# First of two attention stages: row maximum subtracted by TensorE in PSUM, fp16 halves written in two copies, small products alternating between row tiles

## Chip, cores and metric

The kernel runs on one core of a Trainium2 chip. A time is the device time of one execution in microseconds (us), from the first to the last instruction plus what lies around them. The hardware profiler's record of one execution is what this text calls the trace; its span runs from the first to the last instruction.

## What is computed

The input x is (16, 256, 128) in fp32. It passes a windowed self-attention with residual ("first attention"), and then a stack of six layers, each of them a windowed causal attention with 16 heads of 64 and a gated feed-forward (GELU). Only the first attention is touched by the change. Cut to what matters:

```
xn  = layernorm(x)                                  # over the 128 channels
qkv = xn.reshape(64 windows, 64, 128) @ W_qkv       # 16 heads of 8
q, k = layernorm(q) * gamma + beta, layernorm(k) * gamma + beta
attn = softmax((q * 8/8) @ k.T)                     # 64 x 64 per window and head
x   = x + (attn @ v) @ W_proj + b_proj
x   = x + six_layers(layernorm(x))
```

## The kernel before, in words

**Stages of the first attention** (`first_attention`, L298 to L527). The 16 sequences are worked in 8 units of two sequences, that is 4 tiles of 128 tokens (two windows) each. A unit passes six stages: `stage_load` (row statistics by `row_stats`, four transposes on TensorE), `stage_qkv` (three products of 128x384 per tile, then the layernorm of q and k per head), `stage_heads` (q and k are split in an fp16 high half and an fp16 rest, both are written to `hl`, with the halves doubled so that one product of 32 rows holds high*high, high*rest and rest*high, and `hl` is transposed by a DMA), `stage_soft`, `stage_out` and `stage_norm` (second row statistics, transposes into `xg`, the input of the six layers). `stage_soft` and `stage_out` take half a unit (two tiles) at a time, so the first attention is a software pipeline of 16 half-steps, with the later stages of old units beside the early stages of new ones. The loop at the end (`for k in range(2 * NU + LN0)`) merges the stages by fixed offsets.

**In `stage_soft`** each tile has two groups `jj` of scores, one PSUM bank `ps` each. VectorE takes the maximum of the bank (L449) and subtracts it on the way into SBUF, `p0` (L450). ScalarE exponentiates a whole tile (L460) and writes the fp16 high half (L462), GpSimd writes the rest (L463), and a DMA transposes both to `pt` (L465). **In `stage_out`** TensorE multiplies by v (L481, 48 products per tile, all of window c = 0 and then all of c = 1, in two PSUM tiles `po`), VectorE divides by the sums (L483, L486), and TensorE transposes and projects (L494, L501).

**Order.** The kernel is written in the tile framework: its scheduler fixes, when the kernel is built, one order of instructions for each engine, and an engine starts nothing before the instruction ahead of it has started. Nothing in the first attention is pinned; the order follows priorities and the scheduler's own estimates. The six layers have their order on TensorE written out (`pin`). SBUF and PSUM of the first attention are released and used again by the six layers: `SPLIT0 = (2, 2, 2, 1, 1)` gives the PSUM banks of the pools pq, ps, po, py, pt of the first attention, `SPLIT = (2, 3, 2, 1)` those of the six layers, on the same eight banks in the same order. The last stages of the first attention and the first projections of the six layers (`stage_p`, TensorE line L292 with `bank<-wqkv,xhl`) overlap in time.

**The weights** of layer 0 are prepared beside the first attention (`weights(0, ...)`).

The two lines on the maximum before:

```python
V.tensor_reduce(nm, psf, AX.X, ALU.max)                                  # L449
V.tensor_tensor(p0[...], psf, nm.unsqueeze(2).to_broadcast([128, 8, 64]), ALU.subtract)   # L450
```

Of the kernel before, what the change touches and what calls it, by code (L numbers as in the profile page):

```python
# [31 lines left out]
LOAD_AT = 6  # L32
LOAD_T = 10
SPLIT = (2, 3, 2, 1)
SPLIT0 = (2, 2, 2, 1, 1)
USE = dict(p=0, t=1, w=1, s=2, f=3)
USE_V = (1, 2)
LQ0, LH0, LS0, LO0, LN0 = 2, 4, 6, 7, 9
# [18 lines left out]
def kernel(  # L57
# [28 lines left out]

    ident = const.tile([128, 128], F32, name="ident")
    make_identity(nc, ident)
    onesm = const.tile([128, 128], F32, name="onesm")
    G.memset(onesm, 1.0 / 128.0)  # L90
    center = const.tile([128, 128], F32, name="center")
# [203 lines left out]
        pin(T.transpose(*args))  # L295


    def first_attention(p1, p2, p3, pqp, psp0, pop, pyp, ptp=None):  # L298
        ptp = ptp or pyp
        def rsqrt(dst, src, scale):  # L300
            if dst.shape[1] != 128:
                S.activation(dst, src, AF.Ln, bias=epst, scale=scale)
# [13 lines left out]
        def row_stats(xt, pre):  # L316
            mu = p3.tile([128, 4], F32, name=f"{pre}mu")
            rs = p3.tile([128, 4], F32, name=f"{pre}rs")
            sq = p3.tile([128, 128], F32, name="sq0")
            for t in range(4):  # L320
                S.activation(sq, xt[:, t], AF.Copy, scale=-1.0 / 128.0, accum_out=mu[:, t : t + 1])
            for t in range(4):
                S.activation(sq, xt[:, t], AF.Square, bias=mu[:, t : t + 1], accum_out=rs[:, t : t + 1])
            rsqrt(rs, rs, 1.0 / 128.0)
            return mu, rs
# [20 lines left out]
        dma(gam, g0.partition_broadcast(128))  # L346
        dma(bet, be0.partition_broadcast(128))
        dma(bpt, bp0.partition_broadcast(128))
        pm = pqp.tile([128, 512], F32, name="pq")
        T.matmul(pm[:, 0:384], onesm, w0r, start=True, stop=True)  # L350
        V.tensor_tensor(w0r, w0r, pm[:, 0:384], ALU.subtract)
# [13 lines left out]
        def stage_load(u):  # L365
            if u:
                load_x(u)
            e = U[u]
            _, e.rs = row_stats(e.xt, "a")
            e.rv = p1.tile([128, 4], F32, name="rv")  # L370
            V.tensor_scalar(e.rv, e.rs, VPRE, None, ALU.mult)
            yield
            e.xnt = p1.tile([128, 2, 4, 128], FR, name="xnt")
            pt = ptp.tile([128, 4, 128], F32, name="pt" if ptp is not pyp else "py")
            for t in range(4):
                T.transpose(pt[:, t], e.xt[:, t], ident)
            S.copy(e.xnt[:, 0], pt)
            V.tensor_tensor(e.xnt[:, 1], pt, e.xnt[:, 0].bitcast(F32), ALU.subtract)
            G.tensor_tensor(e.xt, e.xt, bpt.unsqueeze(1).to_broadcast([128, 4, 128]), ALU.add)
            yield  # L380
# [26 lines left out]
        def stage_heads(u):  # L407
            e = U[u]
            e.hl = []
            for s in range(2):  # L410
                src = e.qk[:, :, s * 128 : s * 128 + 128].rearrange("p t (h d) -> p t h d", d=8)
                hl = p1.tile([128, 4, 16, 4, 8], HP, name=f"hl{s}")
                for t in range(4):
                    hi, lo = hl[:, t, :, 0], hl[:, t, :, 2 if s else 1]
                    S.copy(hi, src[:, t])
                    G.tensor_tensor(lo, src[:, t], hi, ALU.subtract)
                    if s:
                        V.tensor_copy(hl[:, t, :, 1:4:2], hl[:, t, :, 0:3:2])
                    else:
                        V.tensor_copy(hl[:, t, :, 2:4], hl[:, t, :, 0:2])  # L420
                tr = p2.tile([128, 4, 4, 128], HP, name=f"tr{s}")
                nc.sync.dma_start_transpose(
                    tr.rearrange("p t i q -> p (t i) q"), hl.rearrange("p t h a d -> p (t h a d)")
                )
                e.hl.append(tr)
                yield

        def stage_soft(u, n2):
            e = U[u]
            p0 = p2.tile([128, 2, 8, 128], F32, name="p0")  # L430
            for n in range(2):
                t = 2 * n2 + n
                for jj in range(2):
                    ps = psp0.tile([128, 4, 2, 64], F32, name="ps")
                    for i in range(4):
                        for c in range(2):
                            cols = slice(64 * c, 64 * c + 64)
                            for vp in range(2):
                                r = slice(64 * jj + 32 * vp, 64 * jj + 32 * vp + 32)
                                T.matmul(  # L440
                                    ps[64 * vp : 64 * vp + 64, i, c],
                                    e.hl[0][r, t, i, cols],
                                    e.hl[1][r, t, i, cols],
                                    start=True,
                                    stop=True,
                                )
                    nm = p2.tile([128, 8], F32, name="nm0", bufs=4)
                    psf = ps.rearrange("p i c k -> p (i c) k")
                    V.tensor_reduce(nm, psf, AX.X, ALU.max)  # L449
                    V.tensor_tensor(  # L450
                        p0[:, n, 4 * jj : 4 * jj + 4].rearrange("p i (c k) -> p (i c) k", c=2),
                        psf,
                        nm.unsqueeze(2).to_broadcast([128, 8, 64]),
                        ALU.subtract,
                    )
                    yield
            e.pt = {}
            for n in range(2):
                pf = p0[:, n]
                S.activation(pf, pf, AF.Exp)  # L460
                ph = p2.tile([128, 2, 8, 128], HP, name="ph")
                S.copy(ph[:, 0], pf)  # L462
                G.tensor_tensor(ph[:, 1], pf, ph[:, 0], ALU.subtract)  # L463
                e.pt[n] = p3.tile([128, 16, 128], HP, name="pt0", bufs=3)
                nc.sync.dma_start_transpose(e.pt[n], ph.rearrange("p l m k -> p (l m k)"))  # L465
                yield

        def stage_out(u, n2):
            e = U[u]
            for n in range(2):  # L470
                t = 2 * n2 + n
                pt0 = e.pt[n]
                v = v0[(4 * u + t) % NV0]
                o0 = p3.tile([128, 2, 8, 8], F32, name="o0")
                for c in range(2):
                    r = slice(64 * c, 64 * c + 64)
                    po = pop.tile([128, 8, 18], F32, name="po")
                    for gm in range(8):
                        p = gm % 4 * 2 + gm // 4
                        for q, (a, b) in enumerate(((0, 0), (0, 1), (1, 0))):  # L480
                            T.matmul(po[:, p], pt0[r, a * 8 + gm], v[r, b, p], start=(q == 0), stop=(q == 2))  # L481
                    rc = p3.tile([128, 8], F32, name="rc0")
                    V.reciprocal(rc, po[:, :, 16])  # L483
                    for hp in range(2):
                        h = slice(64 * hp, 64 * hp + 64)
                        V.tensor_tensor(  # L486
                            o0[h, c],
                            po[h, :, hp * 8 : hp * 8 + 8],
                            rc[h].unsqueeze(2).to_broadcast([64, 8, 8]),
                            ALU.mult,  # L490
                        )
                yield
                py = pyp.tile([128, 512], F32, name="py")
                T.transpose(py[:, 0:128], o0.rearrange("p c a b -> p (c a b)"), ident)  # L494
                ot0 = p3.tile([128, 128], F32, name="ot0")
                S.copy(ot0, py[:, 0:128])
                py = pyp.tile([128, 512], F32, name="py")
                for c in range(2):
                    r = slice(64 * c, 64 * c + 64)
                    for hp in range(2):  # L500
                        T.matmul(  # L501
                            py[r, 0:128],
                            ot0[r, hp * 64 : hp * 64 + 64],
                            wp[r, hp],
                            start=(hp == 0),
                            stop=(hp == 1),
                        )
                V.scalar_tensor_tensor(e.xt[:, t], py[:, 0:128], 1.0 / VPRE, e.xt[:, t], ALU.mult, ALU.add)
                yield

        def stage_norm(u):
# [6 lines left out]
            for t in range(4):  # L518
                S.activation(xn[:, t], e.xt[:, t], AF.Identity, bias=mu[:, t : t + 1], scale=rs[:, t : t + 1])
            yield  # L520
            pt = ptp.tile([128, 4, 128], F32, name="pt" if ptp is not pyp else "py")
            for t in range(4):
                T.transpose(pt[:, t], xn[:, t], ident)
            pb = pt.rearrange("p (b j) t -> p b (j t)", j=2)
# [40 lines left out]
    keep = ctx.enter_context(tc.tile_pool(name="keep", bufs=1))  # L565
    work = ctx.enter_context(tc.tile_pool(name="work", bufs=WB))

    identh = keep.tile([128, 128], HP, name="identh")
    V.tensor_copy(identh, ident)
    maskf = keep.tile([128, 256], F32, name="maskf")  # L570
    dma(maskf, masks)
    rowsb = keep.tile([128, 128], BF, name="rowsb")
# [445 lines left out]
```

## Time and profile before

| what | value |
|---|---|
| device time, median of 3 runs | 3251.98 us (3251.57 to 3252.38) |
| device time of the profiled execution | 3248.45 us |
| its span | 3246.6 us |
| last DMA transpose of the first attention has landed, first product of the six layers | 267.9 us, 269.2 us |
| last copy of the first attention into `xg` | 286.4 us |
| busy share of the span: PE, DVE, ACT, POOL | 93%, 80%, 73%, 77% |
| mean granted TensorE clock | 0.957 of full speed |

PE is TensorE's matmuls, PEld its weight loads, DVE is VectorE, ACT is ScalarE, POOL is GpSimd, SP issues DMAs. PEclk is the clock that the throttle granted to TensorE as a share of full speed. A table by stretches gives, for each stretch of the span, every engine's busy time and its number of instructions. A row of a group reads: line, engine, operation, output <- inputs, shapes, count | busy time, mean duration of one in ns | idle time of the engine just before, and who ended it. The first 290 us of the span hold the first attention, the rest the six layers.

### The profile page before, as it was taken

How to read it: one execution, taken by the hardware profiler on the slowest of the kernel's cores; microseconds unless marked ns; L12 is line 12 of the kernel's file. 1: busy time of each engine (PE TensorE's matmuls, PEld its weight loads, DVE VectorE, ACT ScalarE, POOL GpSimd, SP SyncE). 2: the span in 40 equal slices, each digit the busy share in tenths (PEclk: the TensorE clock that was granted, in tenths of full speed). 3: DMA queues.
4: the chain of work that ended last, by engine and by line, in shares of the span. 5: the costliest groups of instructions: out<-in, count | busy, mean ns of one | idle time of the engine just before them, and what ended most of it. 6: DMA issues, size and time to landing. Idle time of an engine off the chain costs nothing. (4 is left out here: it accounts for less than half of the span.)

```text
span 3246.6 us, 153222 instructions
## 1 busy us (share of the span) xinstructions
PE 3016.5 (93%) x67106; PEld 2111.2 (65%) x67106; DVE 2600.2 (80%) x4850; ACT 2379.4 (73%) x5034; POOL 2509.8 (77%) x2578
## 2 busy tenths in 40 slices
PE   4887999999999999999999999999999999999996
PEld 3665766666666666666666666666666666666664
DVE  7987888888788888788887788888788888777783
ACT  6877777777777777777777777777777777767773
POOL 5657988888888888888878888878888888877771
PEclk6558999999999999999999999999999999999998
DMA  4763444444344344344444344444444444443342
GB/s 110 133 130 81 100 102 102 84 85 94 83 102 102 84 85 94 83 102 102 84 85 94 83 102 102 84 85 95 83 105 99 84 85 95 80 100 89 92 92 52
DMA packets 622946, 302.98 MB, mean 93 GB/s; under 512 B 533447, under 2 KB 545733, under 8 KB 622277
## 3 DMA queue, kind: packets, MB, share of 16 engines
q1 hardware_dynamic: 622276, 293.18, 42.9%
q8 instruction: 528, 8.65, 1.1%
q14 instruction: 142, 1.16, 0.1%
HBM read 22.45 MB, written 4.19 MB: 8 GB/s over the span
## 5 line engine op out<-in xcount | busy, mean ns | idle before, releaser
L292 PE MATMUL bank<-wqkv,xhl 128*128 128x512 f16 x3456 | 1238.8, 381 | 8.7 <-ACT sq L653 8.3
L655 POOL TENSOR_TENSOR sum<-mc 128x512 f32<-128x512 f32 x768 | 994.5, 1298 | 256.2 <-DVE mc L644 251.2
L644 DVE TENSOR_TENSOR mc<-bank,tq 128x1024 f32<-128x1024 f32 x768 | 930.1, 1220 | 137.9 <-PE bank L295 128.9
L665 POOL TENSOR_TENSOR sum<-sum,r 128x512 f32<-128x512 f32 x768 | 797.3, 1059 | 32.0
L654 DVE TENSOR_REDUCE r<-sq 128x8 f32<-128x512 f32 x768 | 519.8, 682 | 295.1 <-ACT sq L653 288.1
L295 PE MATMUL bank<-ident,sum 128*128 128x128 f32 x3072 | 713.0, 273 | 23.6 <-DVE of L792 23.6
L797 POOL TENSOR_TENSOR ohl<-of,ohl 128x512 f16<-128x512 f32 x384 | 451.5, 1176 | 225.8 <-ACT ohl L796 225.1
L653 ACT ACTIVATE sq<-bank 128x512 f32<-128x512 f32 x768 | 457.2, 609 | 159.7 <-DVE mc L644 158.2
L295 PEld LDWEIGHTS bank<-ident,sum 128*128 128x128 f32 x3072 | 433.1, 141 | 175.9 <-issue 68.4
L292 PEld LDWEIGHTS <-xhl 128*128 128x128 f16 x3456 | 339.3, 98 | 185.6 <-issue 18.0
L796 ACT CAST ohl<-of 128x512 f16<-128x512 f32 x384 | 237.8, 619 | 283.8 <-DVE of L792 279.9
L292 PE MATMUL bank<-vb,pt 64*32 64x65 f32 x6144 | 389.9, 225 | 31.0 <-ACT pt L622 21.0
L292 PEld LDWEIGHTS bank<-vb,pt 64*32 64x32 f32 x6144 | 263.8, 106 | 191.4 <-ACT p L276 51.7
L295 PE MATMUL bank<-ident,p 128*128 128x128 f32 x1536 | 354.9, 273 | 0.0
L292 PE MATMUL bank<-v,pt 64*32 64x65 f32 x6144 | 320.0, 225 | 35.0 <-ACT gt L282 13.4
L292 PE MATMUL bank<-vw,pt 64*32 64x65 f32 x12288 | 338.1, 225 | 0.1
L292 PE MATMUL bank<-ot,wohl 128*128 128x128 f16 x4608 | 296.0, 222 | 4.5 <-DMA ot<-ohl 4.5
L792 DVE TENSOR_TENSOR of<-bank,rc 128x256 f32<-128x256 f32 x768 | 294.2, 417 | 1.6
L292 PE MATMUL bank<-kt,qt 64*32 64x64 f32 (+1 forms) x24576 | 283.4, 223 | 1.6 <-issue 1.6
L292 PEld LDWEIGHTS bank<-kt,qt 64*32 64x32 f32 x24576 | 255.0, 105 | 45.6 <-issue 45.5
L292 PEld LDWEIGHTS bank<-v,pt 64*32 64x32 f32 x6144 | 237.0, 106 | 66.4 <-ACT pt L622 21.2
L292 PEld LDWEIGHTS <-wohl 128*128 128x128 f16 x4608 | 262.9, 99 | 22.5 <-DMA ot<-ohl 4.7
(155 smaller groups left out, 5063.1 us busy)
## 6 DMA issues: line engine op xcount, KB each, us to landing
v<-vb SPq DMA_DIRECT2D x384, 130.0 KB
vw<-vb SPq DMA_DIRECT2D x384, 130.0 KB
vw<-vb SPq DMA_DIRECT2D x576, 65.0 KB
wraw<-in_L_ffn_Wqkv_dram SPq DMA_DIRECT2D x36, 256.0 KB
wraw<-in_L_ffn_Wo_dram SPq DMA_DIRECT2D x12, 256.0 KB
ot<-ohl SPq DMA_TRANSPOSE x192
xt<-in_L_attn_x_dram SPq DMA_DIRECT2D x8, 256.0 KB
r1d<-xt SPq DMA_DIRECT2D x8, 256.0 KB
```

The lines of the kernel that those rows point to most:

```text
L292: pin(T.matmul(*args, **how))
L295: pin(T.transpose(*args))
L644: V.tensor_tensor(prod, p4.unsqueeze(3).to_broadcast([128, 8, 2, 2, 32]), tq[:, s, d.j].unsqueeze(1).to_broadcast([128, 8, 2, 2, 32]), ALU ...
L653: S.activation(sq, pp.rearrange("p (h d) -> p h d", d=64), AF.Square)
L654: V.tensor_reduce(r[:, hb * 8 : hb * 8 + 8], sq, AX.X, ALU.add)
L655: G.tensor_tensor(mc, m2[:, :, 0], m2[:, :, 1], ALU.add)
L665: G.tensor_tensor(mc, mc, rb.unsqueeze(2).to_broadcast([128, 8, 64]), ALU.mult)
L792: V.tensor_tensor(of[:, :, a], po[a][:, :, 0:64], rc.unsqueeze(2).to_broadcast([128, 4, 64]), ALU.mult)
L796: S.copy(ohl[:, 0, h], of)
L797: G.tensor_tensor(ohl[:, 1, h], of, ohl[:, 0, h], ALU.subtract)
```

## The change

In the first attention only:

- `stage_soft`: the maximum is taken negated in fp16, and TensorE adds it to the scores in PSUM by a product with the fp16 identity (128x512, one per bank); ScalarE exponentiates straight from PSUM, a bank at a time. The fp16 high half is then written by VectorE instead of ScalarE. The two banks of a tile are filled alternately, by four row tiles of 32 instead of two. `ps` has three banks instead of two.
- `stage_heads`: the high half and the rest are each written twice in one instruction (a broadcast source of 256 elements); the VectorE copies that doubled them go. The scale of the scores moves from the exponent's input into gamma and beta (two small GpSimd products) and the activation's scale.
- `stage_out`: the products with v, and the projections, alternate between the two row tiles c; both windows are in one PSUM tile of two banks, `po`, of which there is one; the reciprocal and the two products after it take both windows at once.
- `row_stats`: the sum of the rows by one VectorE reduction and a small GpSimd product instead of four ScalarE passes; `rv` by GpSimd.
- The transposes `pt` of `stage_load` and `stage_norm` take their PSUM from the pool pq, which the projections of the first attention use, instead of a bank of their own: `SPLIT0 = (2, 3, 1, 1)`. `identh` is made at the start instead of after the first attention.

```diff
-SPLIT0 = (2, 2, 2, 1, 1)
+SPLIT0 = (2, 3, 1, 1)
...
-            for t in range(4):
-                S.activation(sq, xt[:, t], AF.Copy, scale=-1.0 / 128.0, accum_out=mu[:, t : t + 1])
+            V.tensor_reduce(mu, xt, AX.X, ALU.add)
+            G.tensor_scalar(mu, mu, -1.0 / 128.0, None, ALU.mult)
...
+        for g in (gam, bet):
+            G.tensor_scalar(g, g, SDIV**-0.5, None, ALU.mult)
...
-            V.tensor_scalar(e.rv, e.rs, VPRE, None, ALU.mult)
+            G.tensor_scalar(e.rv, e.rs, VPRE, None, ALU.mult)
...
-            pt = ptp.tile([128, 4, 128], F32, name="pt" if ptp is not pyp else "py")
+            pt = pqp.tile([128, 512], F32, name="pq").rearrange("p (t c) -> p t c", t=4)
...
+                hi, lo = (slice(0, 2), slice(2, 4)) if s else (slice(0, 3, 2), slice(1, 4, 2))
                 for t in range(4):
-                    hi, lo = hl[:, t, :, 0], hl[:, t, :, 2 if s else 1]
-                    S.copy(hi, src[:, t])
-                    G.tensor_tensor(lo, src[:, t], hi, ALU.subtract)
-                    if s:
-                        V.tensor_copy(hl[:, t, :, 1:4:2], hl[:, t, :, 0:3:2])
-                    else:
-                        V.tensor_copy(hl[:, t, :, 2:4], hl[:, t, :, 0:2])
+                    two = src[:, t].unsqueeze(2).to_broadcast([128, 16, 2, 8])
+                    S.copy(hl[:, t, :, hi], two)
+                    G.tensor_tensor(hl[:, t, :, lo], two, hl[:, t, :, hi], ALU.subtract)
...
-                for jj in range(2):
-                    ps = psp0.tile([128, 4, 2, 64], F32, name="ps")
-                    for i in range(4):
-                        for c in range(2):
+                pss = [psp0.tile([128, 4, 2, 64], F32, name="ps") for jj in range(2)]
+                for i in range(4):
+                    for c in range(2):
+                        for jj in range(2):
                             for vp in range(2):
-                                    start=True,
-                                    stop=True,
+                                    start=(i == 0 and c == 0),
+                                    stop=False,
...
-                    V.tensor_reduce(nm, psf, AX.X, ALU.max)
-                    V.tensor_tensor(p0[...], psf, nm.unsqueeze(2).to_broadcast([128, 8, 64]), ALU.subtract)
+                    V.tensor_reduce(nm, psf, AX.X, ALU.max, negate=True)
+                    T.matmul(psf, identh, nm.unsqueeze(2).to_broadcast([128, 8, 64]), start=False, stop=True)
+                    S.activation(p0[...], psf, AF.Exp, scale=SDIV)
...
-                S.activation(pf, pf, AF.Exp)
-                S.copy(ph[:, 0], pf)
+                V.tensor_copy(ph[:, 0], pf)
                 G.tensor_tensor(ph[:, 1], pf, ph[:, 0], ALU.subtract)
...
-                for c in range(2):
-                    r = slice(64 * c, 64 * c + 64)
-                    po = pop.tile([128, 8, 18], F32, name="po")
-                    for gm in range(8):
-                        for q, (a, b) in enumerate(((0, 0), (0, 1), (1, 0))):
-                            T.matmul(po[:, p], pt0[r, a * 8 + gm], v[r, b, p], ...)
-                    V.reciprocal(rc, po[:, :, 16])
+                both = pop.tile([128, 2, 512], F32, name="po")
+                po = both[:, :, 0:144].rearrange("p c (m e) -> p c m e", e=18)
+                for gm in range(8):
+                    for q, (a, b) in enumerate(((0, 0), (0, 1), (1, 0))):
+                        for c in range(2):
+                            T.matmul(po[:, c, p], pt0[r, a * 8 + gm], v[r, b, p], ...)
+                V.reciprocal(rc, po[:, :, :, 16])
...
-                for c in range(2):
-                    for hp in range(2):
+                for hp in range(2):
+                    for c in range(2):
                         T.matmul(py[r, 0:128], ot0[r, hp * 64 : hp * 64 + 64], wp[r, hp], ...)
...
-    identh = keep.tile([128, 128], HP, name="identh")
-    V.tensor_copy(identh, ident)
```

More of the change, by code (lines that the diff above doesn't have):

```diff
@@ L88 @@
     make_identity(nc, ident)
+    identh = const.tile([128, 128], HP, name="identh")
+    V.tensor_copy(identh, ident)
     onesm = const.tile([128, 128], F32, name="onesm")
@@ L295, in flip, with first_attention @@
         pin(T.transpose(*args))
-    def first_attention(p1, p2, p3, pqp, psp0, pop, pyp, ptp=None):
-        ptp = ptp or pyp
+    def first_attention(p1, p2, p3, pqp, psp0, pop, pyp):
         def rsqrt(dst, src, scale):
@@ L432, in stage_soft @@
                 t = 2 * n2 + n
-                for jj in range(2):
-                    ps = psp0.tile([128, 4, 2, 64], F32, name="ps")
-                    for i in range(4):
-                        for c in range(2):
-                            cols = slice(64 * c, 64 * c + 64)
+                pss = [psp0.tile([128, 4, 2, 64], F32, name="ps") for jj in range(2)]
+                for i in range(4):
+                    for c in range(2):
+                        cols = slice(64 * c, 64 * c + 64)
+                        for jj in range(2):
                             for vp in range(2):
@@ L440, in stage_soft @@
                                 T.matmul(
-                                    ps[64 * vp : 64 * vp + 64, i, c],
+                                    pss[jj][64 * vp : 64 * vp + 64, i, c],
                                     e.hl[0][r, t, i, cols],
                                     e.hl[1][r, t, i, cols],
-                                    start=True,
-                                    stop=True,
-                                )
-                    nm = p2.tile([128, 8], F32, name="nm0", bufs=4)
+                                    start=(i == 0 and c == 0),
+                                    stop=False,
+                                    skip_group_check=True,
+                                )
+                for jj in range(2):
+                    ps = pss[jj]
+                    nm = p2.tile([128, 8], HP, name="nm0", bufs=4)
                     psf = ps.rearrange("p i c k -> p (i c) k")
-                    V.tensor_reduce(nm, psf, AX.X, ALU.max)
-                    V.tensor_tensor(
+                    V.tensor_reduce(nm, psf, AX.X, ALU.max, negate=True)
+                    T.matmul(
+                        psf,
+                        identh,
+                        nm.unsqueeze(2).to_broadcast([128, 8, 64]),
+                        start=False,
+                        stop=True,
+                        skip_group_check=True,
+                    )
+                    S.activation(
                         p0[:, n, 4 * jj : 4 * jj + 4].rearrange("p i (c k) -> p (i c) k", c=2),
                         psf,
-                        nm.unsqueeze(2).to_broadcast([128, 8, 64]),
-                        ALU.subtract,
+                        AF.Exp,
+                        scale=SDIV,
                     )
@@ L474, in stage_out @@
                 o0 = p3.tile([128, 2, 8, 8], F32, name="o0")
-                for c in range(2):
-                    r = slice(64 * c, 64 * c + 64)
-                    po = pop.tile([128, 8, 18], F32, name="po")
-                    for gm in range(8):
-                        p = gm % 4 * 2 + gm // 4
-                        for q, (a, b) in enumerate(((0, 0), (0, 1), (1, 0))):
-                            T.matmul(po[:, p], pt0[r, a * 8 + gm], v[r, b, p], start=(q == 0), stop=(q == 2))
-                    rc = p3.tile([128, 8], F32, name="rc0")
-                    V.reciprocal(rc, po[:, :, 16])
-                    for hp in range(2):
[L485 to L491, printed above, removed]
+                both = pop.tile([128, 2, 512], F32, name="po")
+                po = both[:, :, 0:144].rearrange("p c (m e) -> p c m e", e=18)
+                for gm in range(8):
+                    p = gm % 4 * 2 + gm // 4
+                    for q, (a, b) in enumerate(((0, 0), (0, 1), (1, 0))):
+                        for c in range(2):
+                            r = slice(64 * c, 64 * c + 64)
+                            T.matmul(po[:, c, p], pt0[r, a * 8 + gm], v[r, b, p], start=(q == 0), stop=(q == 2))
+                rc = p3.tile([128, 2, 8], F32, name="rc0")
+                V.reciprocal(rc, po[:, :, :, 16])
+                for hp in range(2):
+                    h = slice(64 * hp, 64 * hp + 64)
+                    V.tensor_tensor(
+                        o0[h],
+                        po[h, :, :, hp * 8 : hp * 8 + 8],
+                        rc[h].unsqueeze(3).to_broadcast([64, 2, 8, 8]),
+                        ALU.mult,
+                    )
                 yield
@@ L497, in stage_out @@
                 py = pyp.tile([128, 512], F32, name="py")
-                for c in range(2):
-                    r = slice(64 * c, 64 * c + 64)
-                    for hp in range(2):
+                for hp in range(2):
+                    for c in range(2):
+                        r = slice(64 * c, 64 * c + 64)
                         T.matmul(
@@ L520, in stage_norm @@
             yield
-            pt = ptp.tile([128, 4, 128], F32, name="pt" if ptp is not pyp else "py")
+            pt = pqp.tile([128, 512], F32, name="pq").rearrange("p (t c) -> p t c", t=4)
             for t in range(4):
```

## The prediction

> **What bounds the kernel now.** I read the page's slices first, to see where the first attention lies and at what clock.
>
> ```profile
> PE   4887999999999999999999999999999999999996
> DVE  7987888888788888788887788888788888777783
> PEclk6558999999999999999999999999999999999998
> ```
>
> Each digit is 81 us. After slice four PE stays at nine tenths at full clock: the six layers, which the diff doesn't touch. All that can change is before that, about 290 us. There PE runs at half clock and DVE is as busy as PE. The table by stretches says more:
>
> ```profile
> 0.00:52.00 52.00, 19.02 (x58) 12.91 (x59) 33.41 (x66) 35.80 (x139) 23.24 (x66) 0.70 0.40 110
> 60.00:207.00 147.00, 120.83 (x2015) 91.52 (x2013) 134.52 (x346) 112.12 (x320) 90.87 (x76) 0.51 0.70 129
> 200.00:210.00 10.00, 10.00 (x164) 8.15 (x161) 9.75 (x31) 6.48 (x20) 3.26 (x2) 0.50 0.36 81
> 207.00:268.00 61.00, 46.10 (x819) 34.01 (x816) 44.80 (x122) 42.07 (x112) 29.85 (x21) 0.50 0.62 118
> 268.00:290.00 22.00, 16.42 (x243) 9.32 (x243) 18.38 (x28) 15.51 (x44) 18.14 (x23) 0.89 0.21 56
> ```
>
> Columns: stretch, length, then PE, PEld, DVE, ACT, POOL busy, clock, DMA. I call them fill (0 to 52), full pipeline (60 to 207, 11.4 half-steps of 12.9), tail (207 to 268: no new units, 4 half-steps of about 13.6) and hand-over. In the full pipeline DVE is 92% busy (134.5 of 147), PE 82%, ACT 76%, POOL 62%: DVE sets the pace. In the tail nobody is above 76%: waits set it. What DVE does, from its groups in 60 to 207:
>
> ```profile
> L450 DVE TENSOR_TENSOR p<-ps,nm 128x512 f32<-128x512 f32 x44 | 29.9, 681 | 0.7
> L449 DVE TENSOR_REDUCE nm<-ps 128x8 f32<-128x512 f32 x43 | 29.5, 686 | 1.7 <-PE ps L440 1.1
> L486 DVE TENSOR_TENSOR o<-po,rc 64x64 f32<-64x64 f32 x84 | 18.2, 217 | 1.1
> L420 DVE COPY hl<-hl 128x256 f16<-128x256 f16 x20 | 8.6, 469 | 1.0 <-POOL hl L416 0.9
> L418 DVE COPY hl<-hl 128x256 f16<-128x256 f16 x20 | 7.5, 386 | 0.2
> ```
>
> The copies' fastest took 0.175 us, their mean is 0.43. The timeline shows why:
>
> ```profile
> 147.85 1.35 POOL L379 TENSOR_TENSOR xt<-xt,bpt 128x512 f32<-128x512 f32 x1 [5.25 <-PE po L481]
> 148.11 2.17 DVE L402 TENSOR_TENSOR qk<-qk,sm 128x1024 f32<-128x1024 f32 x1
> 149.16 3.10 POOL L463 TENSOR_TENSOR ph<-p,ph 128x1024 f16<-128x1024 f32 x1
> ...
> 150.92 1.37 DVE L371 TENSOR_SCALAR rv<-ars 128x4 f32<-128x4 f32 x1
> ```
>
> L402 takes 1.21 us alone; here it started at 148.11 while POOL ran until 149.20, and ended 1.08 later. POOL's next instruction takes 2.13 alone and took 3.10: it stood while L402 ran. L371, four elements a row, ended at 152.29, just after POOL at 152.26. So DVE's SBUF-to-SBUF copies, casts and two-input products take turns with POOL for something that both need; I call it the **shared path**. DVE's reads of PSUM pass freely.
>
> **The change, part by part.** Sums are for the full pipeline, 147 us.
>
> DVE. Off: L450, 43 at 0.63 (back to back a 128x512 pass starts 0.60 to 0.65 after the one before): 27.1. L418 and L420, 16.1 less overlaps: 14.8. L371, 3 at 0.96: 2.9. L486 becomes half as many of twice the size; the 128x128 pass L508 adds 0.26: 84 x 0.195 - 42 x 0.26 = 5.5. L483: 42 x 0.147 - 21 x 0.16 = 2.8. On: the row sums, 11 at 0.64 (the L449 row): 7.0. The cast of `ph`, 22 of 128x1024: a DVE cast of 128x384 took 0.354 (L358) and a one-input pass of 128x128 took 0.22 (L313), so 0.52 ns an element, 0.69, of which 0.63 counts: 13.9. It uses the shared path: its wait is between 0 and 2.1 (the whole L463); POOL will be busy some 70% and its instructions last 1 to 2.3, so I take 0.6: 13. Sum: 134.5 - 53.1 + 33.9 = 115.3, **78%** of the old pace.
>
> PE. On: 43 identity products. The same form in the six layers lies 0.217 after its like at full clock; this stretch is at 0.51, so 0.43, and a change of form costs (the last L440 to the next form 0.166 instead of 0.054, L481 0.101 instead of 0.027): 0.12 more, 23.7 in all; below that 18.5, if it falls on changes that are there anyway. Off: the products with v lie 0.027 apart in one row tile; at 147.57 to 147.64, where the two row tiles happened to mix, 0.0125 apart: 48 per tile, 22 tiles, 14 saved (0 if mixing does nothing at half clock). Scores: pairs of row tiles start together every 0.06, four would halve 26.5; but in the order of the changed kernel the second bank often has to wait for its release, so only about half are mixed: 8 saved (0 to 13). The projection gains nothing: L501's two row tiles already start 0.014 apart. Sum 120.8 + 23.7 - 22 = 122.5, **83%**: unchanged.
>
> The Trainium skill, "TensorE: Matmul & The Clock Gate", Part 1, says that a busy window of about 3.4 us lifts the clock to full. The row 200 to 210 shows PE 10.00 busy of 10.00 at 0.50, so here a busy PE is not enough. By the page PE's sum would halve, to some 61, and the forecast below would be about 4 us lower; the measured row decides, and I keep half clock.
>
> ACT. Off: L462 (21.6), the L321 passes with their read-outs (32 x 0.32 = 10.2). L460's 22.2 becomes 43 passes from PSUM at 0.57 (L276 `p<-bank`: 0.60): 24.5. L415 doubles its elements: 40 x 0.11 (L595, 128x256: 0.405): +4.4. 112 becomes 87, 60%. ACT stops mattering.
>
> POOL. L416 doubles: 0.43 becomes 0.65 (L596, 128x256): 40 x 0.22 = 9. The 14 small products at 0.1 (memsets) to 0.25 (L661): at most 3.4. 90.9 becomes **103**, 70%.
>
> Shared path. Before: POOL 90.9, copies 40 x 0.175 = 7, L402 6, the layernorm chain L308 to L314 6.5: 110, 75%. After: 103.3 + 6 + 6.5 + casts 22 x 0.69 = 15.2: **131, 89%**. That is the new bound: less than DVE's 92%, but not by much. If the fullest resource reaches 93 to 94%, the stretch is 140: **-7** for these, **-8** with the half-step before them. Ends: 100% gives 131 (-16), 86% gives 152 (+5).
>
> Added waits: PE now waits for the maximum 64 times, with `po` products and transposes queued behind; DVE's maximum may stand behind a cast that waits for POOL. That is inside the +5.
>
> Fill: ACT is full from 10 to 30 and loses 20 x 0.32 = 6.4, but the chain to the first score goes over POOL's two L403/L404 and eight L416, which gets 8 x 0.22 longer: **-2** (-5 to 0).
>
> Tail: in the last tile, from the end of L450 (256.9) to the landing (267.9) is 11.0: ACT took L460 at 257.58 and L462 only at 260.36. After: identity product 0.45, Exp 0.6, cast 0.7, L463 2.13, landing 4.3, hops: 8.5. With L450 itself gone: -3; the three half-steps before it at -1.7 each (L450 twice 0.63, no ACT queue for the cast): -5. **-8** (-12 to 0).
>
> Hand-over, which speaks against the change:
>
> ```profile
> 267.89 1.36 PE L481 MATMUL po<-v,pt 64*128 64x18 f16 x48 [1.48 <-DMA pt<-ph]
> 269.18 2.74 PE L292 MATMUL bank<-wqkv,xhl 128*128 128x512 f16 x6
> ...
> 283.30 0.98 PE L523 MATMUL pt<-ident,xn 128*128 128x128 f32 x4
> ```
>
> Now the six layers start 1.3 after the last landing, and the last unit's projection, statistics and transposes (until 284.3) run beside them. Afterwards the last transposes use pq, the banks of the layers' first projections, and in the changed order on PE all of the last unit stands ahead of the first layer product. Its chain alone: products 0.9, mask cast behind its DMA 1.9, L486 0.6, L494, L496 and L501 1.9, L508 and row sum 1.0, POOL 0.3, four squares 2.0, logarithm, exponent and product 0.9, four scalings 1.7, transposes 0.5: 11.7. So the layers start about 10.4 later after the landing, less 1 for a quieter start: **+9.5** (+5, if the layers then catch up on a free POOL, to +11).
>
> Sum: -2 - 8 - 8 + 9.5 = -8.5: 3248.45 becomes 3240. The profiled execution is 3.5 below the runs' median, so from that 3251.98 - 8.5, **3243**.
>
> **Rivals.** (1) Slower: the shared path. Casts wait for POOL, the maxima wait behind them, PE stands at the identity product; full pipeline +5, tail -3, fill 0, hand-over +10: +12, 3264; with half of that 3261. For it: 89% of a path that two in-order engines must meet on. Against: DVE waited 40 times for copies already. It decides once the stages give less than 3 us back against the hand-over's 9.5. (2) Alternating does not do what it says: half-clock pitch stays 0.027 and 0.03; PE is 144 of 147, full pipeline +2, tail -5, fill -2, hand-over 9.5: +4.5; with part of it 3253, no change. (3) Larger: path and DVE fill up to 97% and the tail loses a wait per tile: -4 - 13 - 12 + 6 = -23, 3229.
>
> **How the numbers follow.** Forecast (3234 to 3250) 0.41; (3) 0.24; (1) 0.21; (2) 0.14. About 0.2% (6.5 us) is what this kernel's measurement tells from no change: under 3245.5 is faster, over 3258.5 slower. Forecast: 0.28 faster, 0.13 same; (3) faster; (2) same; (1) 0.20 slower, 0.01 same. Faster 0.52, same 0.28, slower 0.20. The range takes in (3)'s lower half and (1): 3223 to 3263.
>
> **What would show it.** After: no ACT pass of 128x1024 in the first attention; `ph` casts on DVE with a median above 1 us and a fastest near 0.69; products with v near 0.0135 apart; clock still near 0.5 until 270; last landing near 250 instead of 267.9; first layer product some 11 after it instead of 1.3. Wrong, if PE's clock rises early, if the casts never wait, or if the layers overlap the last unit after all.

## The result, and the profile after

The changed kernel takes 3268.14 us (median of 6 runs, 3266.38 to 3269.58) beside 3252.18 for the kernel before (6 runs, 3250.77 to 3252.83): **slower by 0.48%**, ratio 1.0048 with the interval 1.0036 to 1.006. The forecast was 3243, the range 3223 to 3263. The profiled execution took 3269.58, with a span of 3267.8, so the two profiles differ by 21.1, the medians by 16.0: the profiled execution of before was 3.7 below its median, that of after 1.4 above. One execution of ten of a kernel below, b_heads, took 5447 us and is left out of its time; it is the one that was profiled, so no trace of b_heads is used.

First the table by stretches of the changed kernel (length, then busy PE, PEld, DVE, ACT, POOL, clock, DMA), with the same limits as in the prediction:

```profile
0.00:52.00 52.00, 17.43 (x45) 11.77 (x46) 28.31 (x53) 30.48 (x94) 28.33 (x74) 1.00 0.40 109
60.00:207.00 147.00, 117.50 (x1941) 76.84 (x1942) 107.80 (x214) 88.23 (x261) 107.00 (x87) 0.55 0.66 127
207.00:268.00 61.00, 51.91 (x882) 32.01 (x880) 44.60 (x86) 32.43 (x91) 30.27 (x22) 0.50 0.60 113
268.00:290.00 22.00, 8.15 (x128) 5.11 (x129) 3.75 (x13) 7.05 (x22) 4.76 (x9) 0.50 0.19 45
```

The 1.00 of the fill is no sign of a faster clock: the trace's first clock record comes at 55.6 us, and what lies ahead of the first record reads as 1.00. In b_banks below, whose trace has no record before 298.9, the first layer products (at 296.1) lie 0.427 apart as in before at 0.50, where they fall to 0.215 with the clock at 1.00.

In the full pipeline (60 to 207) VectorE fell from 92% to 73%, ScalarE from 76% to 60%, PE went from 82% to 80%, GpSimd rose from 62% to 73%. **Nobody is above 80%, and still the work goes no faster.** The stretch of the hand-over, 268 to 290, is nearly empty: PE 8.15 of 22, before 16.42.

The same moments of both traces, from PE's and VectorE's rows in time (a half-step is two tiles; the 64 maxima span 15.75 half-steps):

| moment, us of the span | before | after | later by |
|---|---|---|---|
| first product of scores | 52.4 | 53.7 | 1.3 |
| last maximum starts | 255.5 | 262.9 | 7.4 |
| last tile's products with v start (its transposition has landed) | 267.9 | 276.3 | 8.4 |
| first product of the six layers | 269.2 | 289.4 | 20.2 |
| end | 3246.6 | 3267.8 | 21.2 |
| pace, per half-step, from first to last maximum | 12.85 | 13.20 | 0.35 |

So there are two losses: 8.4 until the last landing, and 11.8 between it and the layers. What the engines waited for in 60 to 207 (engine, line, releaser: us in total, times, longest):

```profile
POOL ph L473 <- DVE ph L472: 18.8, 11, 4.7
PE po L492 <- DMA pt<-ph: 18.6, 10, 3.1
ACT p L461 <- PE ps L453: 18.3, 14, 2.5
```

The same waits before:

```profile
POOL ph L463 <- ACT ph L462: 44.6, 11, 7.8
ACT p L460 <- DVE p L450: 15.5, 10, 3.7
PE po L481 <- DMA pt<-ph: 3.8, 4, 1.2
```

GpSimd waits less for the cast than before, 18.8 instead of 44.6. ScalarE waits 18.3 for identity products (L453), where it waited 15.5 for the subtraction. New is that PE stands 18.6 for landings instead of 3.8. How that looks for one tile, in the rows of the timeline (start, length, engine):

```profile
160.01 1.29 DVE L452 TENSOR_REDUCE nm<-ps 128x8 f16<-128x512 f32 x2
...
161.48 0.61 PE L453 MATMUL ps<-nm,identh 128*128 128x512 f16 x1
...
162.33 1.11 PE L512 MATMUL py<-wp,ot 64*64 64x128 f32 x8
162.49 2.55 ACT L419 CAST hl<-qk 128x256 f16<-128x256 f32 x8
...
163.38 0.59 PE L492 MATMUL po<-v,pt 64*128 64x18 f16 x31
163.91 0.61 PE L453 MATMUL ps<-nm,identh 128*128 128x512 f16 x1
164.44 5.52 POOL L420 TENSOR_TENSOR hl<-qk,hl 128x256 f16<-128x256 f32 x8
165.07 0.60 ACT L461 ACTIVATE p<-ps 128x512 f32<-128x512 f32 x1
165.95 0.58 ACT L461 ACTIVATE p<-ps 128x512 f32<-128x512 f32 x1
166.62 0.93 DVE L472 CAST ph<-p 128x1024 f16<-128x1024 f32 x1 [0.17 <-ACT p L461]
169.92 2.13 POOL L473 TENSOR_TENSOR ph<-p,ph 128x1024 f16<-128x1024 f32 x1
```

Both maxima are there at 161.30. The second identity product comes at 163.91, behind a projection and the products with v of one tile (2, 15 and 31 of its 48); the exponents at 165.07 and 165.95, behind eight casts of `stage_heads` on ScalarE; the rest `ph` at 169.92, behind the doubled rests L420 on GpSimd. Over all 64 banks the identity product starts 1.53 after the end of its maximum, and PE is idle for only 0.21 of that; before, the subtraction started 0.55 after it. A step that came on VectorE right behind its maximum now stands in PE's queue.

The hand-over, PE's rows:

```profile
276.25 0.81 PE L492 MATMUL po<-v,pt 64*128 64x18 f16 x48 [2.46 <-DMA pt<-ph]
279.62 0.45 PE L505 MATMUL py<-ident,o 128*128 128x128 f32 x1 [2.55 <-DVE o L497]
280.47 1.12 PE L512 MATMUL py<-wp,ot 64*64 64x128 f32 x8 [0.41 <-ACT ot L507]
286.49 1.63 PE L534 MATMUL pq<-ident,xn 128*128 128x128 f32 x4 [4.90 <-ACT xn L530]
289.38 2.72 PE L294 MATMUL bank<-wqkv,xhl 128*128 128x512 f16 x6 [1.26 <-ACT xg L537]
```

This is the forecast's chain: all of the last unit, with PE idle between, and the first layer product only after the copy that frees the bank.

### The profile page after: what moved, and what is told of

It reads as the page before. It is cut to its first block, busy times and chain, and to the rows that moved or that the text cites. A ratio compares the mean times of both kernels' runs of the same rounds, so it can differ in the third digit from the quotient of the medians.

```text
span 3267.8 us, 153096 instructions
## 1 busy us (share of the span) xinstructions
PE 3026.8 (93%) x67170; PEld 2097.7 (64%) x67170; DVE 2568.0 (79%) x4666; ACT 2342.8 (72%) x4906; POOL 2537.5 (78%) x2604
## 5 line engine op out<-in xcount | busy, mean ns | idle before, releaser
L294 PE MATMUL bank<-ot,wohl 128*128 128x128 f16 x4608 | 296.1, 222 | 4.5 <-DMA ot<-ohl 4.5
L631 ACT COPY kt<-bank 128x512 f32<-128x512 f32 x384 | 226.7, 590 | 71.7 <-PE bank L297 68.0
```

The source lines that it names most:

```text
L294: pin(T.matmul(*args, **how))
L631: S.copy(to[:, mb * 4 : mb * 4 + 4], hold[0])
```

## The experiments

The theories by their letters: **H**, the hand-over; **S**, the path that VectorE's SBUF passes share with GpSimd; **Q**, **I**, **W**, the identity product in PE's queue; **T**, PE's load at half clock; **B**, the banks of the transposes; **L**, latency between stages; **P**, GpSimd's queue. Every run was timed beside the kernel before on the same chip, whose median was 3250.1 to 3253.4; differences are taken against that one. Kernels named a_ start from the changed kernel, b_ from the one before. One table for all; busy shares are those of 60 to 207, the hand-over is the time from the start of the last tile's `po` products to the first layer product.

| kernel | us above before | ratio to before (interval) | pace | PE, DVE, ACT, POOL % | hand-over |
|---|---|---|---|---|---|
| before |  |  | 12.85 | 82, 92, 76, 62 | 1.3 |
| after | +16.0 | 1.0048 (1.0036 to 1.006) | 13.20 | 80, 73, 60, 73 | 13.1 |
| b_banks | +26.5 | 1.0078 (1.0062 to 1.0093) | 13.87 | 73, 85, 72, 58 | 12.5 |
| a_norm_py | +7.5 | 1.0023 (1.0013 to 1.0033) | 13.08 | 83, 75, 61, 73 | 0.7 |
| a_act_cast | +17.4 | 1.005 (1.0033 to 1.0067) | 12.98 | 73, 60, 73, 70 | 15.2 |
| a_pt_own | +15.0 | 1.0049 (1.0034 to 1.0064) | 13.91 | 81, 68, 59, 71 | 0.8 |
| a_both_py | +14.9 | 1.0047 (1.0032 to 1.0062) | 13.07 | 75, 74, 57, 72 | -5.1 |
| b_pq_ps2 | +9.1 | 1.0028 (1.0018 to 1.0038) | 13.10 | 80, 88, 76, 61 | 12.5 |
| b_ident | +18.9 | 1.0064 (1.0047 to 1.0081) | 14.09 | 84, 71, 72, 58 | 1.3 |
| a_lag2 | +24.5 | 1.0077 (1.0062 to 1.0093) | 13.16 | 78, 78, 62, 75 | 12.8 |
| a_heads | +12.1 | 1.0041 (1.0026 to 1.0055) | 13.29 | 78, 82, 56, 63 | 13.2 |
| b_alt | -5.2 | 0.9986 (0.9977 to 0.9996) | 12.71 | 71, 88, 75, 62 | 0.8 |
| b_heads | -0.5 | 0.9999 (0.999 to 1.0009) |  |  |  |
| a_dve_sub | +19.2 | 1.0057 (1.0042 to 1.0072) | 13.16 | 66, 92, 59, 69 | 13.6 |
| b_alt_ident | +14.0 | 1.0042 (1.0027 to 1.0057) | 13.54 | 81, 73, 73, 61 | 0.8 |
| b_zero | +18.4 | 1.0055 (1.004 to 1.007) | 13.89 | 86, 87, 73, 58 | 1.3 |
| b_alt_heads | -13.9 | 0.9957 (0.9943 to 0.9971) | 11.96 | 77, 85, 83, 74 | 1.5 |
| b_ahi | +3.0 | 1.0009 (0.9999 to 1.0018) | 13.21 | 80, 62, 79, 70 | 0.8 |
| b_rest | -2.7 | 0.999 (0.998 to 0.9999) | 12.74 | 71, 92, 59, 73 | -1.0 |

**The bank of the transposes.** b_banks and b_pq_ps2 make only this edit on the kernel before, with and without the third bank for `ps`; a_norm_py undoes half of it.

```diff
-SPLIT0 = (2, 2, 2, 1, 1)
+SPLIT0 = (2, 3, 2, 1)                            # b_banks; b_pq_ps2: (2, 2, 2, 1)
-pt = ptp.tile(...)                               # stage_load, stage_norm
+pt = pqp.tile([128, 512], F32, name="pq")...
```

> The kernel before with one edit: the transposes of stage_load and stage_norm take their PSUM from pq, and ps has the third bank (SPLIT0 = 2, 3, 2, 1). Theory H (hand-over): the last unit's transposes now stand ahead of the six layers on PE, because they use the layers' banks; the first layer product comes 9 to 13 us after the last landing instead of 1.3, and the time is 8 to 12 us above before, 3260 to 3264. Theory Q (PE's queue: the changed kernel loses in the full pipeline, because the identity product puts the softmax behind products with v that wait for their transposed input): this kernel has no identity product, so it is within 3 us of before, 3249 to 3255.

> The kernel before with the transposes in pq and nothing else: ps keeps two banks (SPLIT0 = 2, 2, 2, 1, one bank unused). Theory B: as b_banks, 3274 to 3281. Rival: the third bank of ps shifted the scheduler's order in b_banks and cost the pace; then only the hand-over is left, 3260 to 3264.

In both the layers start 12.5 after the last landing: H holds, and b_pq_ps2 is 9.1 above before, as H says. Every kernel of the table with the last transposes in pq has 12.5 to 15.2 there, every other one 1.5 or less. But b_banks is 17.4 slower than b_pq_ps2, and its pace 13.87 instead of 13.10, for one **more** bank of scores. No work was added: PE has 67106 products in both. They stand in another order from the first tiles on (the 84th product is the first that differs, at 51 us), and so do the transpositions on SP. SP's rows of b_banks (start, length):

```profile
157.16 3.96 SPq L422 DMA_TRANSPOSE tr<-hl  x2
161.17 0.58 SPq L514 DMA_DIRECT2D r1d<-xt  x1
167.47 0.38 SPq L335 DMA_DIRECT2D xt<-in_L_attn_x_dram  x1
172.80 14.76 SPq L465 DMA_TRANSPOSE pt<-ph  x3
191.02 3.81 SPq L422 DMA_TRANSPOSE tr<-hl  x2
```

From one unit's `tr` to the next one's pass 33.9 us here. A single interval says little (before has one of 33.0 too); the five intervals from the third unit's `tr` to the last one's take 162.2 in b_banks, 145.7 in b_pq_ps2 and 140.0 in before. With one more free bank and the same instructions, the order that the scheduler fixed is what is left to explain these 17 us; that is argued, since no run held the order fixed. So one step between two of these kernels, even of 17 us, can come from the order, and a step is read as a cause only where several kernels show it.

a_norm_py:

```diff
-            pt = pqp.tile([128, 512], F32, name="pq")...    # stage_norm
+            pt = pyp.tile([128, 512], F32, name="py")...
```

> The changed kernel, with the transposes of stage_norm taken from the bank py of the projection, not from pq. Theory H: the layers start again 1 to 3 us after the last landing; 9 to 12 us faster than the changed kernel, 3256 to 3259, with the last landing still near 276. Theory Q: the hand-over is worth 3 us or less, 3265 to 3268.

PE's rows of a_norm_py at the hand-over:

```profile
272.96 0.81 PE L492 MATMUL po<-v,pt 64*128 64x18 f16 x48 [0.72 <-DMA pt<-ph]
273.71 3.07 PE L294 MATMUL bank<-wqkv,xhl 128*128 128x512 f16 x6
278.02 1.48 PE L534 MATMUL py<-ident,xn 128*128 128x128 f32 x4 [1.24 <-ACT xn L530]
```

PE goes from the last `po` into the layers, and the transposes of the last unit come after. The time is 8.5 below the changed kernel by the table (9.3 in the medians as they stand, 3258.8 beside 3268.1), near the least that H said (9), and far from Q's 3 or less. The layers start 15.7 earlier but end only 7.2 earlier in the profiles: the last unit's transposes now run until 301.4 beside them. Of the loss, 7.5 us are left.

**The shared path.** a_act_cast: `V.tensor_copy(ph[:, 0], pf)` becomes `S.copy(ph[:, 0], pf)`.

> The changed kernel, with the fp16 high half cast by ScalarE as before, not by VectorE. Theory S: 22 casts leave the shared path, which falls from 89% to 79%; the last scores come 5 to 8 us earlier, and the time falls by as much. Theory Q: the pace is set by latency along PE's queue, a cast of 1.05 on ScalarE instead of 1.06 on VectorE changes it by less than 3 us.

The time did not move (3268.6 beside 3268.1). VectorE is 60% busy now, the pace 12.98, and the last scores end 2.5 earlier, where S asked for 5 to 8. S falls as what alone bounds the changed kernel.

**Other banks.** a_pt_own gives both transposes their own bank again (`SPLIT0 = (2, 2, 1, 1, 1)`), a_both_py puts both in py.

> The changed kernel with its transposes of stage_load and stage_norm in a bank of their own as before, and ps with two banks (SPLIT0 = 2, 2, 1, 1, 1). Theory B (banks: transposes in pq hold up the projections of stage_qkv, and the units with them, besides the hand-over): 16 to 25 us below the changed kernel, 3243 to 3252, with the last landing at 262 to 268. Theory Q (identity products in PE's queue set the pace): only the hand-over comes back, 3256 to 3260, as in a_norm_py, with the last landing near 274.

> The changed kernel with both transposes in py, ps still with three banks. Theory B: pq is free of them, 3243 to 3252. Theory Q: as a_norm_py, 3256 to 3260. A third case: the one bank of py becomes the new hold-up, over 3262.

Both have the early hand-over, and both lose it again: a_pt_own by a pace of 13.91 (probably since its two banks of scores are filled together, so that the next tile finds none free), a_both_py by a drain in which the last tile's `po` products start 26.8 after the last scores (253.9 to 280.7; after: 15.2). B says too much: the transposes cost the hand-over, not the pace.

**One more half-step of lag.** a_lag sets `LO0, LN0 = 8, 10` and adds buffers.

> The changed kernel, with stage_out and stage_norm one half-step later (LO0, LN0 = 8, 10) and the buffers that this needs (pt0 5, xt 6, v0 16). Theory Q: the products with v no longer wait for a landing (18.6 us of PE idle between 60 and 207 become under 6), the last scores start near 245 to 252 instead of 260.7, and the time is 5 to 12 us below the changed kernel. Theory S (the path that DVE's SBUF passes share with POOL sets the pace): the path carries the same work, the last scores stay near 260, the time is within 3 us of the changed kernel or above it.

This edit did not do what it says. A unit keeps one list of transposed tiles for both halves, so the products of its first half read those of its second half, and had to wait for them (3279.1, ratio 1.0085, interval 1.007 to 1.01). Nothing follows from it. a_lag2 keeps the halves apart (`e.pt[2 * n2 + n]`, read as `e.pt[t]`):

> The changed kernel with stage_out one half-step further behind stage_soft and stage_norm one behind its place (LO0, LN0 = 8, 10), each half's transposed tiles kept apart, and the buffers that this needs (pt0 5, xt 6, v0 16). Theory L (no engine is full; the pace is latency: products with v stand in PE's queue for their landing, and what is behind them waits): the 18.6 us that PE waited for landings in 60 to 207 fall under 6 and the last scores come near 245 to 252 instead of 260.7; the time falls 5 to 12 us, to 3256 to 3263. Theory P (GpSimd's own queue is the chain): the last scores stay within 4 us of 260.7, and the extra half-step adds 0 to 10 us at the end, 3268 to 3278.

The waits of `po` for landings are gone from PE, as expected, but the last scores are at 260.6 and the time is 8.5 above the changed kernel, as P expected. So these waits were where PE's slack showed, not what made it slow. L falls.

**The doubled writes.** a_heads and b_heads exchange only this part of `stage_heads`:

```diff
-S.copy(hl[:, t, :, hi], two);  G.tensor_tensor(hl[:, t, :, lo], two, hl[:, t, :, hi], ALU.subtract)
+S.copy(hi, src[:, t]);  G.tensor_tensor(lo, src[:, t], hi, ALU.subtract);  V.tensor_copy(...)
```

> The changed kernel with stage_heads' copies as before: each half written once by ScalarE and GpSimd, doubled by VectorE. Theory P: followed back from the last products with v, the changed kernel's chain from 60 to 276 lies 81 us on GpSimd, 27 of them in the doubled rests; halving them takes 10 to 12 us off GpSimd in 60 to 207, and the last landing comes 5 to 10 us earlier, 3258 to 3264. Theory L: within 3 us of the changed kernel, 3265 to 3271.

> The kernel before with the doubled writes of stage_heads alone. VectorE loses 40 copies, 14.8 us of 134.5, GpSimd gains some 11. By the sum of the prediction, where VectorE sets the pace, 7 to 12 us below before, 3241 to 3246. Theory P: GpSimd's chain (heads, then the softmax's rests) takes it back, within 3 us of before or up to 6 above.

a_heads gains 3.9 by the table (3264.8 beside 3268.1 as they stand), less than P wants and within the two intervals; b_heads nothing. GpSimd's queue may be part of the chain; that it sets the pace is not shown. Of b_heads only the time is used.

**The alternation.** b_alt takes over `stage_out` alone.

> The kernel before with the alternating products alone: stage_out as in the changed kernel, po of two banks once, all banks else as before. By the prediction's terms DVE loses 8.3 us of 134.5 and PE 14 of 120.8 in the full pipeline, and DVE sets the pace: 6 to 10 us below before, 3242 to 3247. If the single po tile makes PE wait for VectorE's two products instead: within 3 us of before or above it.

5.2 below before: this part is a gain, though of a size that the order alone could make. PE's own time in products with v from 60 to 207, from each start to the next product's start or its own end, falls from 32.3 (1056 of them) to 18.0 (1008).

**The identity product.** b_ident adds it alone to the kernel before:

```diff
-V.tensor_reduce(nm, psf, AX.X, ALU.max)
-V.tensor_tensor(p0[...], psf, nm..., ALU.subtract)
-S.activation(pf, pf, AF.Exp)
+V.tensor_reduce(nm, psf, AX.X, ALU.max, negate=True)
+T.matmul(psf, identh, nm..., start=False, stop=True)
+S.activation(p0[...], psf, AF.Exp)
```

> The kernel before with the identity product alone: negated fp16 maximum, product in PSUM, exponent from PSUM by banks; the high half stays on ScalarE, banks, heads and products with v as before. By the sums of the prediction DVE loses 27 us of 147 and PE gains 24 and becomes 97% busy: 0 to 8 us above before, 3251 to 3260. Theory Q: the softmax also waits in PE's queue, 8 to 20 above, 3260 to 3272. Theory B says nothing of it.

The table by stretches of b_ident (columns as before):

```profile
60.00:207.00 147.00, 123.39 (x1764) 84.43 (x1758) 104.23 (x268) 105.84 (x321) 84.58 (x73) 0.53 0.62 118
207.00:268.00 61.00, 56.23 (x908) 38.29 (x908) 40.18 (x112) 39.68 (x104) 27.35 (x20) 0.51 0.58 108
```

VectorE is down to 71%, and yet the pace is 14.09 instead of 12.85: 18.9 us slower. In the stretch after 207 PE is 92% busy. Two kernels take the cause apart: b_zero adds a product of the same size, by zeros, **ahead** of the maximum (PE's work without a wait for VectorE), b_alt_ident gives PE room first.

```diff
+T.matmul(psf, identh, zero..., start=False, stop=True)      # b_zero
 V.tensor_reduce(nm, psf, AX.X, ALU.max)
```

> The kernel before, with an identity product of the same size that adds zeros to each bank of scores straight after them, ahead of the maximum; VectorE subtracts as before. PE has the work of the identity product, but waits for no maximum. Theory T: 12 to 20 us above before, 3264 to 3272. Theory W: VectorE still sets the pace and the product is 0.46 of latency, 2 to 7 above, 3254 to 3259.

> The kernel before with the alternating products and the identity product, no other part. The alternation takes 14 us off PE in 60 to 207. Theory T (the identity product costs because PE at half clock becomes full): PE has room for it again, PE's sum is 128 of 147, 3247 to 3254. Theory W (it costs because the softmax then stands in PE's in-order queue twice a tile, whatever PE's load): b_alt plus the 15 to 20 us that it cost alone, 3262 to 3268.

b_zero is 18.4 slower: work on PE costs it, without any wait for a maximum. That is T. But b_alt_ident is 14.0 above before where b_alt is 5.2 below it, 19 for the identity product, although the alternation had freed 14 us of PE: that is W (16.5 in the medians as they stand; the two ran on different chips). **Neither holds alone.** What both share is 64 products of 0.38 (b_zero) to 0.50 (b_alt_ident) each, counted in the same way from 60 to 207, between the scores and the exponent, together 25 to 32; 17 to 19 of it come out in the time, on before twice, on b_alt and, below, on b_alt_heads. Four kernels agree on it, which the order alone would hardly do. Their full pipelines, b_zero first, then b_alt_ident:

```profile
60.00:207.00 147.00, 126.19 (x1904) 87.70 (x1906) 128.35 (x313) 107.12 (x303) 85.25 (x66) 0.55 0.67 115
60.00:207.00 147.00, 118.34 (x1894) 78.99 (x1891) 106.84 (x233) 107.77 (x330) 89.97 (x76) 0.52 0.71 125
```

**In the changed kernel** a_dve_sub takes the identity product out again (subtraction by VectorE, exponent of a whole tile from SBUF):

> The changed kernel with the maximum subtracted by VectorE into SBUF as before, and the exponent over a whole tile from SBUF; all else as changed. Theory I (the identity product is what costs the pace: b_ident alone was 19 above before): the last landing comes near 262 to 268 instead of 276 and the time 8 to 14 us below the changed kernel, 3254 to 3260; the 10 us of the hand-over stay. By the prediction's sums VectorE gets 27 us back on top of the casts, 142 of 147 busy, and sets the pace: 3272 to 3280.

Its full pipeline in the table by stretches:

```profile
60.00:207.00 147.00, 97.70 (x1864) 70.67 (x1862) 135.95 (x255) 86.11 (x231) 101.04 (x80) 0.77 0.65 121
```

(The 0.77 is again for want of a record before 136.7; products with v lie 0.014 apart on both sides of it.) No gain: 3269.3 beside 3268.1. VectorE is at 92% again: the subtractions are back, and the casts and the row sums stand where the copies were. That PE's work sets the pace with the identity product, and VectorE without it, fits this and is not shown: in the changed kernel itself, taking the identity product out gains nothing, so its price there is not known.

**What the other parts are worth.**

> The kernel before with the alternating products and the doubled writes of stage_heads, nothing else: a candidate for a faster kernel. The two alone were 5 us and 0 below before. If VectorE is the bound once PE is relieved: 3240 to 3246. If the parts only add: 3246 to 3249. If GpSimd's doubled writes lie on the chain: 3250 to 3256.

> b_alt_heads (3236) with the identity product added. It cost 19 us on before and 16.5 on b_alt. If that is its price whatever the rest does: 3250 to 3256. If it is worth more where VectorE has less to do (VectorE was 85% busy in b_alt_heads): a small gain or nothing, 3230 to 3239.

> All parts of the change but the identity product, the pairing of the two banks of scores and the edit of the banks: alternating products, doubled writes, row sums by VectorE, rv by GpSimd, the cast of the high half by VectorE. If the identity product carries the loss of the pace: 3234 to 3244. If VectorE becomes the bound (casts 24 and row sums 7 more, on 125 of 147): 3246 to 3258.

b_alt_heads is 13.9 below before, ratio 0.9957: **the fastest kernel of the study**, faster than both. Its full pipeline:

```profile
60.00:207.00 147.00, 112.67 (x2105) 82.58 (x2107) 125.11 (x257) 121.71 (x342) 108.63 (x80) 0.50 0.75 135
```

Four engines between 74 and 85%, pace 11.96. On it the identity product costs 16.9 (b_ahi), the casts and row sums on VectorE 11.2 (b_rest). The parts do not add: -13.9 with 16.9, 11.2 and 9 of the hand-over would be +23, the changed kernel is +16.

One more step can be read from the table. b_rest and a_dve_sub differ only by the edit of the banks (with the third bank of scores), the filling of both score banks together, and the scale that moved into gamma and beta: 21.9 us, at the same 92% of VectorE. The hand-over accounts for about 9. The other 13 are not split, and the order can have its part in them: no run fills the two banks together without the rest. By this path, from b_rest over a_dve_sub to the changed kernel, the banks and their filling cost 21.9 and the identity product nothing.

## Why the prediction was wrong

- **Fill, -2**: +1.3 measured. Small, and wrong in sign.
- **The sizes** were near: DVE 107.8 (forecast 115.3), PE 117.5 (122.5), ACT 88.2 (87), POOL 107.0 (103) of 147; the casts 0.68 at the fastest and 1.065 in the mean, their median 0.83, not above 1. Within a run of products with v the starts lie 0.014 apart in the mean (0, 0.007, 0.020 or 0.027; before 0.026), as forecast; with the change to the next form each takes 0.020 instead of 0.031.
- **Full pipeline and tail, -8 each**: +7.4 at the last maximum, +8.4 at the last landing. The step that failed is "If the fullest resource reaches 93 to 94%, the stretch is 140". It let the fullest resource set the pace, and PE's work therefore cost nothing as long as PE was "83%: unchanged". What took 147 us before took 151 (147 x 13.20 / 12.85) instead of 140, with no engine above 80%. The runs put a price on the work: PE's 64 zero products alone cost 18.4 on the kernel before (b_zero), at VectorE 87% and PE 86%, the identity products 16.9 to 19.2 on three kernels without the edit of the banks. Relief of VectorE, the counterpart of the sum, was worth far less than its time while PE kept its work: 27 us off it in b_ident bought nothing that could be seen, 15 us in b_heads nothing either. After the alternation the same 15 us gained 8.7 (b_alt_heads beside b_alt).
- **The last tile**, in the tail: from the end of the maximum to the landing 8.5 were forecast, 12.6 measured (263.6 to 276.3). The second identity product starts 1.5 after the maximum, and the landing comes 6.1 after the rest, not 4.3.
- **The shared path as the new bound**, and rival (1) with it: the time of rival (1) was the nearest, but its mechanism alone is not the cause. By the forecast's own sum, with GpSimd's measured 107.0 (107.0 + 6 + 6.5 + 15.2), the path came to 135 of 147, 92%; yet with the casts off it the time did not move (a_act_cast).
- **Hand-over, +9.5**: right. 11.8 in the traces, 8.5 and 9.1 by the two kernels that isolate it.
- **Rival (2)**, that the alternation does nothing, was wrong: the starts lie 0.014 apart instead of 0.026, and b_alt is 5.2 below before.
- **The range** ended at 3263 because the full pipeline was allowed +5 at most and the tail was still given 3 us back. An added product in every bank should have been allowed its own length: 64 x 0.46, 29 us, as the far end.

What stays open: why 17 to 19 of the 25 to 32 us appear in the time with PE at 80 to 86%. Load alone (b_alt_ident) and the wait alone (b_zero) are both refuted, and the scheduler's order, to which the third bank points with 17 us, changes with every edit. A run with the order held fixed was not made. Open too is the changed kernel's own share: of its 16 us the hand-over is shown to cost 8.5 to 9, and how the rest divides between the identity product, the third bank and the filling of two score banks together is not.

## What to carry to other kernels

In a pipeline with a fixed order on every engine and nobody full, the busy share of an engine is no room for new work: price an operation that is moved into the chain by up to its own length on the new engine (here 17 to 19 of 25 to 32 us), not at nothing. Look first at whose PSUM banks the last work of one stage holds when the next stage begins with the same banks: that part was computed right and cost 9 of the 16 us. Make the parts of such a change one by one: here two of them, alone worth 5 us and 0, give 14 together, and one costs 19.

## What the runs showed of the hardware

- At half clock, alternating row tiles still help the small products with v: 0.014 from start to start within a run instead of 0.026, and 0.018 to 0.020 each in the mean, the change to the next form included, instead of 0.031. The projections, which alternated every second product already, stayed at 0.130 each.
- The Trainium skill, "TensorE: Matmul & The Clock Gate", Part 1, lets a busy window lift the clock. Here it did not: b_ident kept PE 92% busy from 207 to 268 at 0.51. In the changed kernel the clock was 0.55 in the full pipeline, with four short rises of 3.4 us, and it was back at full only at 301.3, 12 us after the first layer product; before, 3.7 after it.
- From their first product to the end the six layers take 2976 to 2982 us in most of these kernels (before 2977.4, after 2978.4). Where the last unit's transposes end more than 20 us after that first product it is 2985 to 2987 (a_norm_py, a_pt_own, a_both_py, b_rest): so much of the last unit beside the layers goes with some 8 us more in them, in one profiled execution of each.
